# Sums moved to TensorE, projections and sorting moved into other stages, in a four-layer graph kernel

## The chip, the cores and the metric

The kernel runs on one core of a Trainium2 chip. The metric is the device time of one execution in microseconds. The kernel before was run three times: median 3336.72 us, from 3329.15 to 3339.13. One further execution was profiled.

Engines are named as the profile names them: PE is TensorE (PEld its weight loads), DVE is VectorE, ACT is ScalarE, POOL is GpSimd, SP is SyncE, which here only issues DMAs.

## What is computed

A graph of N = 2708 nodes with 128 features passes through four layers. Each has the form x = x + layer(relu(layernorm(x)), adj); everything is fp32. The adjacency `adj` is 2708 x 2708 with some five entries in a row.

```python
# layer 0: graph convolution with symmetric scaling
fc = h @ W + b;  d = adj.sum(1)
x += (adj * d**-.5[:, None] * d**-.5[None, :]) @ fc
# layer 1: attention; here d = 128 "heads" of width h = 8
q = (h @ Wq.T).reshape(d, n, 8)          # k and v alike
a = einsum('dnh,dmh->dnm', q, k) * d**-.5 + adj + adj
x += einsum('dnm,dmh->dnh', softmax(a, 2), v).reshape(n, 8 * d) @ Wo.T
# layer 2: mean over in-edges, two linear maps, batch norm, relu
# layer 3: gated sum over neighbours
gi = sigmoid(a[None] + b[:, None] + b1) * adj[:, :, None]
x += einsum('ijf,jg->ig', gi, h) @ weight + bias
```

## The kernel before

**Layer 0** passes twice over the adjacency in tiles of 128 rows (22 tiles, the last of 20 rows). The first pass loads every tile, sums its rows (`deg`), scales `fc` by the inverse root, and already transposes and multiplies the first `STAY = 8` tiles; the second pass loads the other 14 again, transposes them (`turned`, L303) and multiplies (`product`, L469). On DVE, `neighbours` finds the up to 16 entries of each row (value and column), for ten tiles in the first pass and twelve in the second. The layer norm of layer 1 (`normed_rows`) runs behind the second pass and leaves the transposed `hT`.

**Projections and sorting** are a stage of their own. 144 products of 128 x 512 (L641) make q, k and v; ACT (L648) and DVE (L650) evict them in turn into two tiles, and six DMAs store them to `qkv_c` in DRAM. Beside it `in_order` computes each row's place when rows are sorted by their number of neighbours, and 22 indirect DMAs on POOL's queue scatter the records to `list_d` (L612). Rows sorted so need only `ROOM[t]` neighbour slots in tile t, 121 in all.

**The loop over heads** is written out by hand (`manual_schedule`): engines get their instructions in the order of the code. Exp of the small logit is replaced by a polynomial, so a head's attention over all nodes is a matrix of moments: 128 features of k (`fk`) times nine moments by nine values (`y`), summed over nodes (`moments`, L1200), weighted (L1210), and multiplied with the transposed features of q. The transposes (`turn`, L1226) go through the one PSUM bank of `ps_t` and an ACT copy (`fT`, L1228); `evaluate` multiplies (L1238), scales the 81 results per node by the moments of q (L1246, DVE) and sums nine into one (L1252, DVE). A head has six such chunks of up to four row tiles, and features of the next two heads are made beside it by `keys` (mostly POOL), `with_values` (`y`) and `queries` (DVE). After every fourth head `sums` adds the sum of all v (from `prepare`, L806 to L817) on POOL (L824) and stores the group.

In the same loop a generator `first` takes 1.5 steps per chunk. It relays q, k, v by node (`by_node`), loads the sorted records (`sorted_rows`), and then handles the 121 neighbour slots (`from_neighbours`), each in six steps: an indirect load of k and v, the product k times q (`logits`, POOL L930), its sum over the eight components (`summed`, DVE L936), Exp and weight (`weigh`, ACT), weight times v (`values`, DVE L954), and a sum into PSUM by products with the identity (`added`, PE L971):

```python
nc.tensor.matmul(accs[t][:sz, j], ident[:sz, :sz], z[:sz, j].rearrange("p c k -> p (c k)"), ...)
```

When `first` is exhausted, `normalise` (add the neighbours' part, divide) and `project_out` (PE L676, with `woT` from `load_wo`) take its place. **Layers 2 and 3** follow and are not touched.

Of the kernel before, what the change touches and what calls it, by code (L numbers as in the profile page):

```python
# [28 lines left out]
STAY = 8  # L29
# [16 lines left out]
def gnn4_kernel(  # L46
# [82 lines left out]
    def neighbours(t, sz, a, pool, seg0, at48):  # L129
# [41 lines left out]
        )  # L171
        yield
        col = pool.tile([P, KS], FP, name="n_col")
        nc.vector.reduce_sum(col[:sz], hot[:sz], axis=AX.X)
# [80 lines left out]
    pre = ExitStack()  # L255
    bp = pre.enter_context(tc.tile_pool(name="l01", bufs=1))
    hT = bp.tile([C, N], FP, name="hT")
    with ExitStack() as ph:
        lp = ph.enter_context(tc.tile_pool(name="l0", bufs=1))
        hp = ph.enter_context(tc.tile_pool(name="l0_h", bufs=3))  # L260
        np_ = ph.enter_context(tc.tile_pool(name="l0_n", bufs=2))
# [4 lines left out]
        pa = ph.enter_context(tc.tile_pool(name="l0_pa", bufs=1, space=PSUM))  # L266

        def by_head(src, name):

            nat = ap.tile([P, KC, C], FP, name=f"{name}_nat", tag="a_nat")  # L270
            nc.sync.dma_start(nat, src.rearrange("(t p) c -> p t c", p=P))
            dst = bp.tile([P, HEAD, C], FP, name=name)
            for i0, iw in _cuts(KC, 4):
                pt = ps.tile([P, BK], FP, name="w_ps", tag="tr")
                for i in range(iw):
                    nc.tensor.transpose(pt[:, i * P : (i + 1) * P], nat[:, i0 + i], ident)
                c0, cw = i0 * P // HEAD, iw * P // HEAD
                nc.vector.tensor_copy(
                    dst[:, :, c0 : c0 + cw],
                    pt[:, : iw * P].rearrange("p (c h) -> p h c", h=HEAD),  # L280
                )
            return dst
# [5 lines left out]
        def rows_of_adj(t):  # L288
            r0, sz = rows[t]
            a = ap.tile([P, N], FP, name="a_nat", tag="a_nat")  # L290
            nc.sync.dma_start(a[:sz], adj[r0 : r0 + sz])
            return a

        def turned(t, a, both):

            sz = rows[t][1]
            at = tp.tile([P, NT, P], FP, name="a_tr")
# [16 lines left out]
        fc = lp.tile([P, NT, C], FP, name="fc")  # L314
        junk = lp.tile([P, N], BF, name="junk")
        mv = lp.tile([P, NT, 2], FP, name="mv_0")
        nc.gpsimd.memset(mv, 1.0)
        with tc.manual_schedule():
            stay, gone = list(range(STAY)), list(range(STAY, NT))
            order = [t for two in zip(stay, gone) for t in two] + gone[STAY:]  # L320
            early = stay + gone[:2]
            wT = [by_head(w, f"wT{i}") for i, w in enumerate((wq, wk, wv))]
            nat = [rows_of_adj(t) for t in order[:3]]
            for t, (_, sz) in enumerate(rows):
                st = hp.tile([P, nc.vector.BN_STATS_DIM], FP, name="ln_st")
                nc.vector.bn_stats(st[:sz], x_sb[:sz, t])
                nc.vector.bn_aggr(mv[:sz, t], st[:sz])
            rstd = lp.tile([P, NT], FP, name="rstd_0")
            nc.scalar.activation(rstd, mv[:, :, 1], AF.Sqrt, bias=eps)
            nc.vector.reciprocal(rstd, rstd)  # L330
            for t0, tw in _cuts(NT, 4):
# [3 lines left out]
                for t in range(t0, t0 + tw):  # L335
                    sz = rows[t][1]
                    h = hp.tile([P, C], FP, name="h_0", bufs=4)
                    nc.vector.tensor_scalar(
                        h[:sz], x_sb[:sz, t], mv[:sz, t, 0:1], rstd[:sz, t : t + 1],
                        ALU.subtract, ALU.mult,  # L340
                    )
                    nc.scalar.activation(h[:sz], h[:sz], AF.Relu)
                    o = (t - t0) * P
                    nc.tensor.transpose(pt[:, o : o + sz], h[:sz], ident[:sz, :sz])
                nc.scalar.copy(hT[:, s0 : s0 + w], pt[:, :w])
            for t, (r0, sz) in enumerate(rows):
                pf = pm.tile([P, C], FP, name="fc_ps", tag="mm")
                nc.tensor.matmul(pf[:sz], hT[:, r0 : r0 + sz], w0_sb, start=True, stop=False)
                nc.tensor.matmul(pf[:sz], ones[0:1, :sz], b0_sb, start=False, stop=True)
                nc.scalar.copy(fc[:sz, t], pf[:sz])  # L350

            sums0 = [pa.tile([P, 4, C], FP, name=f"l0_s{g}") for g in range(-(-STAY // 4))]
# [18 lines left out]
            seg_i = lp.tile([P, SEG, 8], I32, name="seg_i")  # L371
            nc.gpsimd.iota(seg_i, pattern=[[seg_w, SEG], [0, 8]], base=0, channel_multiplier=0)
            seg0 = lp.tile([P, CAND], FP, name="seg0")
            nc.gpsimd.tensor_copy(seg0, seg_i.rearrange("p s e -> p (s e)"))
            at_i = lp.tile([P, CAND], I32, name="at_i")
            nc.gpsimd.iota(at_i, pattern=[[1, CAND]], base=0, channel_multiplier=0)
            at48 = lp.tile([P, CAND], FP, name="at48")
            nc.gpsimd.tensor_copy(at48, at_i)
            found = []

            def look(n):
                for _ in range(n):
                    while found and next(found[0], "done") == "done":
                        found.pop(0)

            seen = []
            for i, t in enumerate(order):
                r0, sz = rows[t]
                if i + 3 < NT:
                    nat.append(rows_of_adj(order[i + 3]))  # L390
                a = nat[i]
                look(3)
                nc.scalar.activation(
                    junk[:sz], a[:sz], AF.Copy, accum_out=deg[:sz, t : t + 1]
                )
                d = dinv[:sz, t : t + 1]
                nc.scalar.activation(d, deg[:sz, t : t + 1], AF.Sqrt)
                nc.vector.tensor_scalar_add(d, d, 1e-8)
                nc.vector.reciprocal(d, d)
                nc.vector.tensor_scalar_mul(fc[:sz, t], fc[:sz, t], d)  # L400
# [5 lines left out]
                products(8 if t in stay else 14)  # L406
                seen.append(t)
                ready += [(j, t) for j in sorted(there)]
                ready += [(t, m) for m in seen[:-1] if t in stay]
            look(6)  # L410
            nat = [rows_of_adj(t) for t in gone[:3]]
            products(len(ready))
# [6 lines left out]
            rs1 = lp.tile([P, NT], FP, name="rs1")  # L419
            normed = []  # L420

            def normed_rows(t0, tw):

                hg = hp.tile([P, 4, C], FP, name="h_1", bufs=2)
                for t in range(t0, t0 + tw):
                    sz = rows[t][1]
                    st = hp.tile([P, nc.vector.BN_STATS_DIM], FP, name="ln_st")
                    nc.vector.bn_stats(st[:sz], x_sb[:sz, t])
                    nc.vector.bn_aggr(mv[:sz, t], st[:sz])
                yield  # L430
                r = rs1[:, t0 : t0 + tw]
                nc.scalar.activation(r, mv[:, t0 : t0 + tw, 1], AF.Sqrt, bias=eps)
                yield
                nc.vector.reciprocal(r, r)
                for t in range(t0, t0 + tw):
                    sz = rows[t][1]
                    nc.vector.tensor_scalar(
                        hg[:sz, t - t0], x_sb[:sz, t], mv[:sz, t, 0:1], rs1[:sz, t : t + 1],
                        ALU.subtract, ALU.mult,
                    )  # L440
                for t in range(t0, t0 + tw):
                    sz = rows[t][1]
                    nc.scalar.activation(hg[:sz, t - t0], hg[:sz, t - t0], AF.Relu)
                yield
                pt = ps.tile([P, BK], FP, name="ln_ps", tag="tr")
                s0 = rows[t0][0]
                w = rows[t0 + tw - 1][0] + rows[t0 + tw - 1][1] - s0
                for t in range(t0, t0 + tw):
                    sz = rows[t][1]
                    o = (t - t0) * P  # L450
                    nc.tensor.transpose(pt[:, o : o + sz], hg[:sz, t - t0], ident[:sz, :sz])
                nc.scalar.copy(hT[:, s0 : s0 + w], pt[:, :w])
                yield

            def norm(n):
                for _ in range(n):
                    while normed and next(normed[0], "done") == "done":
                        normed.pop(0)

            groups = _cuts(NT, 4)  # L460
            while groups and sum(groups[0]) <= STAY:
                normed.append(normed_rows(*groups.pop(0)))
# [11 lines left out]
            def added(t, po):  # L474
# [5 lines left out]
                if groups and sum(groups[0]) == t + 1:  # L480
                    normed.append(normed_rows(*groups.pop(0)))
# [13 lines left out]
            for t in range(STAY, NT):  # L495
                if t + 3 < NT:
                    nat.append(rows_of_adj(t + 3))
                a = nat[t - STAY]
                sz = rows[t][1]
                if t not in early:  # L500
                    found.append(neighbours(t, sz, a, np_, seg0, at48))
                    look(2)
                there[t] = turned(t, a, False)
                if t - STAY + 1 < STAY:
# [4 lines left out]
                )  # L509
                if t > STAY:  # L510
                    pos[t - 1] = product(t - 1)
                if t - 2 in pos:
                    added(t - 2, pos.pop(t - 2))
                look(3)
                norm(2)
# [5 lines left out]
            while normed:  # L521
                norm(1)

    VW = HEAD + 1
    QKV = 3 * HEAD + 1
# [1244 lines left out]
```

## Time and profile before

| what | value |
|---|---|
| median of three runs | 3336.72 us |
| profiled execution | 3354.19 us |
| its span, first to last instruction | 3352.4 us |
| mean granted clock of PE | 0.89 |
| busy: PE, PEld, DVE, ACT, POOL | 80, 68, 66, 39, 60% |
| first head's weighting (L1210) starts | 562.6 us |
| the 25th, the 105th and the last | 970.4, 2353.4, 2814.4 us |

The profiled execution is 17.5 us slower than the median; its stages are used for working, and its own time is what they add up to. Busy PE in the profile is modelled: a matmul's record reaches to the end of its pipeline, so distances between starts say more than durations. In a row of costly groups stand the line, engine and operation, output and inputs with their shapes, the count, then busy time in us and mean duration in ns, and last the idle time of that engine just before, with what ended it. In a table by stage, each engine has its busy time and, in brackets, its instructions.

### The profile page before, as it was taken

To read this page: it belongs to the slowest core of one execution; us is meant where nothing else is said; L and a number is where in the kernel's file an instruction comes from. 1 tells how busy PE (TensorE), PEld (TensorE's weight loads), DVE (VectorE), ACT (ScalarE), POOL (GpSimd) and SP (SyncE) were. 2 spreads that over 40 slices of the span, in tenths; PEclk is the share of its full clock that TensorE was granted. 3 is DMA by queue.
4 is the path that set the end of the run, shared out by engine and by line. 5 is a ranking of instruction groups with operands and counts; after the bars stand their busy time and mean duration, and the time that the engine had idled before them with its cause. 6 is when DMAs were issued, how large, how long until landed. Compare 5 with 4: busy or idle time off the path is not lost. (4 is left out here: it accounts for less than half of the span.)

```text
span 3352.4 us, 50866 instructions
## 1 busy us (share of the span) xinstructions
PE 2691.7 (80%) x17781; PEld 2273.0 (68%) x17781; DVE 2202.7 (66%) x5135; ACT 1314.8 (39%) x3127; POOL 2009.3 (60%) x2263
## 2 busy tenths in 40 slices
PE   6477884888789999999999999999888897796044
PEld 4476543777788887888888788877777886443033
DVE  3868753666678888888888788887666675213222
ACT  3485462555544444444444444444322232102010
POOL 0111115555588888888988888889656663000775
PEclk6688896999999999999999999999888999895565
DMA  3452274777743333333334333343465712541322
GB/s 113 175 227 93 76 326 128 208 214 206 211 131 114 125 125 127 128 132 128 119 138 139 126 141 125 137 143 121 94 148 143 166 48 64 193 176 56 106 83 61
DMA packets 312741, 462.08 MB, mean 138 GB/s; under 512 B 159650, under 2 KB 234404, under 8 KB 289330
## 3 DMA queue, kind: packets, MB, share of 16 engines
q1 hardware_dynamic: 280870, 289.79, 28.3%
q0 software_dynamic: 31600, 168.86, 14.7%
q8 instruction: 148, 2.42, 0.3%
q14 instruction: 123, 1.01, 0.1%
HBM read 344.89 MB, written 113.67 MB: 137 GB/s over the span
## 5 line engine op out<-in xcount | busy, mean ns | idle before, releaser
L1238 PE MATMUL g_ps<-mw,fT 128*128 128x128 f32 x5632 | 817.5, 287 | 155.2 <-ACT fT L1228 115.1
L1238 PEld LDWEIGHTS g_ps<-mw,fT 128*128 128x128 f32 x5632 | 715.4, 196 | 290.6 <-ACT fT L1228 178.4
L1228 ACT COPY fT<-f_ps 128x512 f32<-128x512 f32 (+1 forms) x768 | 420.6, 548 | 1216.7 <-PE f_ps L1226 1216.6
L1200 PE MATMUL m_ps<-y,fk 128*128 128x128 f32 (+1 forms) x5632 | 768.2, 280 | 0.0
L1200 PEld LDWEIGHTS m_ps<-y,fk 128*128 128x128 f32 (+1 forms) x5632 | 699.9, 194 | 15.4
L1150 POOL TENSOR_TENSOR y<-bk,raw 128x792 f32<-128x792 f32 x256 | 415.8, 1624 | 432.1 <-ACT y L1181 420.3
L1246 DVE TENSOR_TENSOR z<-g_ps,bq 128x324 f32<-128x324 f32 (+1 forms) x768 | 355.6, 463 | 435.0 <-PE g_ps L1238 433.6
L1226 PE MATMUL f_ps<-ident,fq 128*128 128x128 f32 x2816 | 441.6, 276 | 14.4 <-DVE v_sum L817 9.3
L1252 DVE TENSOR_REDUCE o_raw<-z 128x36 f32<-128x324 f32 (+1 forms) x768 | 355.8, 463 | 26.4
L1150 POOL TENSOR_TENSOR fk<-bk,raw 128x352 f32<-128x352 f32 (+1 forms) x384 | 357.7, 955 | 0.1
L1226 PEld LDWEIGHTS f_ps<-ident,fq 128*128 128x128 f32 x2816 | 340.2, 144 | 16.2 <-DVE v_sum L817 10.6
L1150 POOL TENSOR_TENSOR fk<-raw,bk 128x352 f32<-128x352 f32 (+1 forms) x512 | 312.6, 640 | 3.1 <-ACT bk L719 2.3
L1147 DVE TENSOR_TENSOR fq<-bq,kq_ps 128x528 f32<-128x528 f32 (+1 forms) x512 | 288.2, 605 | 0.0
L930 POOL TENSOR_TENSOR c_z<-c_kv,c_q 128x1024 f32<-128x1024 f32 (+1 forms) x121 | 284.2, 2349 | 2.2 <-DMA c_kv<-kv_n,srt 1.4
L971 PE MATMUL v_ps<-c_v,ident 128*128 128x512 f32 (+1 forms) x484 | 233.3, 605 | 15.3 <-ACT c_acc L986 15.3
L1591 POOL DMA_INDIRECT g<-gate_d,srt x121 | 120.4, 995 | 110.2 <-issue 109.0
L1147 DVE TENSOR_TENSOR fq<-kq_ps,bq 128x352 f32<-128x352 f32 (+1 forms) x512 | 171.9, 378 | 0.0
L155 POOL CAST n_fl<-n_ci 128x40 f32<-128x40 int32 (+1 forms) x22 | 4.8, 218 | 251.9 <-DVE n_ci L138 251.9
L936 DVE TENSOR_REDUCE c_c<-c_z 128x128 f32<-128x1024 f32 (+1 forms) x121 | 147.5, 1219 | 3.4 <-POOL c_z L930 3.2
L954 DVE TENSOR_TENSOR c_v<-c_kv,c_c 128x1024 f32<-128x1024 f32 (+1 forms) x121 | 146.7, 1212 | 0.0
L971 PEld LDWEIGHTS v_ps<-c_v,ident 128*128 128x128 f32 (+1 forms) x484 | 82.0, 189 | 79.1 <-issue 58.8
L915 POOL DMA_INDIRECT c_kv<-kv_n,srt x121 | 117.8, 974 | 23.1 <-issue 9.6
(290 smaller groups left out, 3714.1 us busy)
## 6 DMA issues: line engine op xcount, KB each, us to landing
a_nat<-in_adj_dram SPq DMA_DIRECT2D x34, 1354.0 KB
qkv_c<-qkv SPq DMA_DIRECT2D x5, 6400.0 KB
a<-in_adj_dram SPq DMA_DIRECT2D x21, 1354.0 KB
kv_n<-n_kv SPq DMA_DIRECT2D x16, 1344.0 KB
o_g<-o_raw SPq DMA_DIRECT2D x32, 396.0 KB
q_n<-n_q SPq DMA_DIRECT2D x16, 672.0 KB
o_cr<-o_c SPq DMA_DIRECT2D x21, 512.0 KB
r_raw<-o_g SPq DMA_DIRECT2D x22, 396.0 KB
```

Source lines behind the costliest of these rows:

```text
L930: nc.gpsimd.tensor_tensor(zs[b][:sz], kvs[b][:sz, 0, :, 0], qs[t][:sz], ALU.mult)
L936: nc.vector.reduce_sum(cs[b][:sz], zs.pop(b)[:sz], axis=AX.X)
L954: nc.vector.tensor_tensor(z[:sz], kv[:sz, 0, :, 1].rearrange("p (j c) k -> p j c k", j=2), c.rearrange("p (j c) -> p j c", j=2)[:, :, :, None]
L971: nc.tensor.matmul(accs[t][:sz, j], ident[:sz, :sz], z[:sz, j].rearrange("p c k -> p (c k)"), start=s0 == 0, stop=s0 == ROOM[t] - 1,)
L1147: nc.vector.tensor_tensor(o, x, y, ALU.mult)
L1150: nc.gpsimd.tensor_tensor(o, x, y, ALU.mult)
L1200: nc.tensor.matmul(pms[d][:, :P], fks[d][:sz, t], ys[d, h][:sz, m * VW * B_ALL : m * VW * B_ALL + P], start=t == 0, stop=t == NT - 1,)
L1226: nc.tensor.transpose(pt[:, m], fqs[d][:, t0 + m], ident)
L1228: nc.scalar.copy(fts[d, c][:, :n], pt[:, :n])
L1238: nc.tensor.matmul(pg[:, m], ft[:, m], mws[d], start=True, stop=True,)
L1246: nc.vector.tensor_tensor(z[:, :n], pg[:, :n, : B_ALL * VW].rearrange("p t (k b) -> p t k b", k=VW), bqs[d % 2][:, t0 : t0 + n, None, :B_A ...
L1252: nc.vector.reduce_sum(ros[g][:, t0 : t0 + n, i], z[:, :n], axis=AX.X,)
```

## The change

- `STAY` becomes 6, so the second pass has 16 tiles. Loads of the adjacency run four tiles ahead, and two tiles of the first pass lie between groups of the first layer norm. Norms subtract and scale on POOL, and ACT scales `fc`.
- Projections move into the second pass: when two row tiles of x are complete, `row_group` norms and transposes them, and `projected` makes q, k and v of one row tile with 24 products of 128 columns, evicts four of them at a time, and stores the tile. The stage of its own goes.
- `in_order` moves into the loop and takes its steps beside those of `by_node`; one scatter each two steps.
- `evaluate` writes the scaled results of half a head into one tile `z`, laid out by the nine moments, and `add_up` sums the nine with products with the identity, once in a head, for the second half of the head before and the first half of this one. Two ACT copies take the sums from PSUM, through the bank of `ps_m`.
- `logits` writes its product by component, and `summed` adds the eight components with products with the identity, through the bank of `ps_t`; Exp reads PSUM.
- The sum of all v is made by products with ones in `all_values` from the relaid tiles, and enters each node's result by a product with a row of ones (`vrow`) that opens the sum over neighbours; the store adds N to the denominator. `sums` goes.
- One more pair of features goes from POOL to DVE, `fT` has two buffers instead of three, `c_z`, `c_v` and `z` get a pool of their own, `load_wo` runs when normalising begins, and in `neighbours` three adds on POOL halve the last sum before DVE reduces it.

```diff
-STAY = 8
+STAY = 6
 def neighbours(t, sz, a, pool, seg0, at48):
...
+        while w % 2 == 0:
+            w //= 2
+            nc.gpsimd.tensor_tensor(
+                hot[:sz, :, :w], hot[:sz, :, :w], hot[:sz, :, w : 2 * w], ALU.add
+            )
...
-        nc.vector.reduce_sum(col[:sz], hot[:sz], axis=AX.X)
+        nc.vector.reduce_sum(col[:sz], hot[:sz, :, :w], axis=AX.X)
...
+            early = stay + gone[STAY + 1 :: 2][:4]
...
+            for n, (t0, tw) in enumerate(_cuts(NT, 4)):
+                turned_rows(t0, tw, scaled(t0, tw))
+                if n in (1, 3):
+                    front(n // 2, None)
...
+            def projected(t):
+                r0, sz = rows[t]
+                ot = ots[t % 2]
+                for i in range(3):
+                    for e0 in range(0, HEAD, 4):
+                        pq = pa.tile([P, 4, P], FP, name="qkv_ps", tag="s")
+                        for e in range(4):
+                            nc.tensor.matmul(
+                                pq[:, e, :sz], wT[i][:, e0 + e], hT[:, r0 : r0 + sz],
+                                start=True, stop=True,
+                            )
+                        yield
+                        scale = (C**-0.5, 1.0, 1.0)[i]
+                        to = ot[:, :sz, i * HEAD + e0 : i * HEAD + e0 + 4]
+                        src = pq[:, :, :sz].rearrange("p e r -> p r e")
+                        turns[0] += 1
+                        if turns[0] % 2:
+                            nc.scalar.mul(to, src, scale)
+                        else:
+                            nc.vector.tensor_scalar_mul(to, src, scale)
+                nc.sync.dma_start(qkv_c[:, r0 : r0 + sz], ot[:, :sz])
+                yield
+            def row_group(t0, tw):
+                stats(t0, tw)
+                yield
+                spread(t0, tw)
+                yield
+                hg = scaled(t0, tw)
+                yield
+                turned_rows(t0, tw, hg)
+                yield
+                for t in range(t0, t0 + tw):
+                    yield from projected(t)
...
             for t in range(STAY, NT):
...
+                go(1)
                 there[t] = turned(t, a, False)
+                go(2)
...
+                go(3)
                 if t > STAY:
                     pos[t - 1] = product(t - 1)
+                go(2)
...
-                norm(2)
+                go(3)
...
-                        pq = pm.tile([P, BK], FP, name="qkv_ps", tag="mm")
-                        nc.tensor.matmul(
-                            pq[:, :cw], wT[i][:, e], hT[:, c0 : c0 + cw], start=True, stop=True
-                        )
...
-                    m, of = (mul2, kh2) if w == 6 and h else (mul, kh)
+                    m, of = (mul2, kh2) if w == 6 else (mul, kh)
...
-            nc.gpsimd.tensor_tensor(
-                ro, ro, vs[:, None].to_broadcast([P, NT, GRP, VW]), ALU.add
-            )
+        def all_values(kv, j):
+            pt = ps_t.tile([P, BK], FP, name="v_t", tag="tr")
+            w = 2 * GRP * HEAD
+            to = pt[0:1, :w].rearrange("p (j i k) -> p j i k", j=2, k=HEAD)
+            for t, (_, sz) in enumerate(rows):
+                nc.tensor.matmul(
+                    to, ones[:sz, 0:1], kv[:sz, t, :, :, 1], start=t == 0, stop=t == NT - 1
+                )
+            nc.scalar.copy(vrow[:, (j // 2) * w : (j // 2 + 1) * w], pt[0:1, :w])
...
+                yield
+                yield
+        def side_by_side(a, b):
+            for _ in a:
+                next(b, None)
+                yield
+            yield from b
...
             def summed(b):
-                cs[b] = c_two[:, b % 2, 0]
-                nc.vector.reduce_sum(cs[b][:sz], zs.pop(b)[:sz], axis=AX.X)
+                z = zs.pop(b)
+                cs[b] = ps_t.tile([P, BK], FP, name="c_l", tag="tr")[:, :C]
+                for k in range(HEAD):
+                    nc.tensor.matmul(
+                        cs[b][:sz], ident[:sz, :sz], z[:sz, k],
+                        start=k == 0, stop=k == HEAD - 1,
+                    )
...
                 if s0 == 0:
                     accs[t] = ps_v.tile([P, 2, BK], FP, name="v_ps")
+                    for j in range(2):
+                        nc.tensor.matmul(
+                            accs[t][:sz, j],
+                            ones[0:1, :sz],
+                            vrow[:, j * BK : (j + 1) * BK],
+                            start=True,
+                            stop=False,
+                        )
...
-        first = chain(by_node(), sorted_rows(), from_neighbours())
+        first = chain(side_by_side(by_node(), in_order()), sorted_rows(), from_neighbours())
...
         def evaluate(d, c):
-            z = tm.tile([P, 4, VW, B_ALL], FP, name="z")
+            if t0 == parts[h][0]:
+                zt[d, h] = tz.tile([P, B_ALL, TM, VW], FP, name="z")
+            m0 = t0 - parts[h][0]
             nc.vector.tensor_tensor(
-                z[:, :n],
+                zt[d, h][:, :, m0 : m0 + n].rearrange("p b t k -> p t k b"),
                 pg[:, :n, : B_ALL * VW].rearrange("p t (k b) -> p t k b", k=VW),
                 bqs[d % 2][:, t0 : t0 + n, None, :B_ALL].to_broadcast([P, n, VW, B_ALL]),
                 ALU.mult,
             )
-            nc.vector.reduce_sum(
-                ros[g][:, t0 : t0 + n, i],
-                z[:, :n],
-                axis=AX.X,
-            )
+        def add_up(which):
+            which = [(d, h) for d, h in which if 0 <= d < D]
+            ps = ps_m.tile([P, BK], FP, name="o_ps", tag="m_ps")
+            at = 0
+            for d, h in which:
+                T = parts[h][1] - parts[h][0]
+                z = zt.pop((d, h))
+                for b in range(B_ALL):
+                    nc.tensor.matmul(
+                        ps[:, at : at + T * VW],
+                        ident,
+                        z[:, b, :T],
+                        start=b == 0,
+                        stop=b == B_ALL - 1,
+                    )
+                at += T * VW
...
+                nc.scalar.copy(
+                    ros[g][:, t0:t1, i],
+                    ps[:, at : at + T * VW].rearrange("p (t k) -> p t k", k=VW),
+                )
...
+                    if c == NCH - 1:
+                        add_up([(d - 1, 1), (d, 0)])
```

## The prediction

> **What bounds the kernel now.** I read the stages first, cut at the starts of the work that names them: both passes over the adjacency, projections and sorting (to 563), 24 heads beside the relayout (to 970), 80 heads beside the neighbours (to 2353), 24 heads beside normalising (to 2829), layers 2 and 3. "Head" below means one pass of the loop over the 128 heads; its start is L1210, which runs once per head.
>
> ```profile
> core 0: us, PE busy (x) PEld busy (x) DVE busy (x) ACT busy (x) POOL busy (x), PEclk, DMA share, GB/s
> 0.00:211.00 211.00, 124.99 (x658) 107.35 (x659) 123.58 (x400) 99.93 (x178) 28.51 (x90) 0.68 0.49 180
> 211.00:380.00 169.00, 127.47 (x954) 116.88 (x953) 132.78 (x406) 103.84 (x188) 29.51 (x62) 0.87 0.24 85
> 380.00:563.00 183.00, 125.77 (x354) 63.95 (x352) 91.03 (x144) 79.40 (x92) 43.89 (x57) 0.82 0.57 225
> 563.00:970.00 407.00, 338.48 (x2664) 318.09 (x2664) 263.82 (x636) 221.05 (x497) 238.99 (x321) 0.94 0.70 192
> 970.00:2353.00 1383.00, 1295.39 (x9348) 1117.01 (x9349) 1143.84 (x2459) 600.35 (x1619) 1209.61 (x1261) 0.99 0.37 129
> 2353.00:2829.00 476.00, 402.78 (x2919) 378.79 (x2918) 312.86 (x700) 149.68 (x385) 283.66 (x303) 0.94 0.46 110
> ```
>
> The long stage has PE at 94%, POOL at 87, DVE at 83. Busy PE is modelled, so I ask next what rate PE keeps where nothing holds it: weight loads of one head in the timeline.
>
> ```profile
> 1505.77 0.97 PEld L1238 LDWEIGHTS g_ps<-mw,fT 128*128 128x128 f32 x8 [0.91 <-ACT fT L1228]
> 1506.65 0.47 PEld L1226 LDWEIGHTS f_ps<-ident,fq 128*128 128x128 f32 x4
> 1507.09 0.97 PEld L1200 LDWEIGHTS m_ps<-y,fk 128*128 128x128 f32 x8
> ...
> 1511.28 0.19 PEld L971 LDWEIGHTS v_ps<-c_v,ident 128*128 128x128 f32 x1 [0.24 <-issue]
> 1511.71 0.19 PEld L971 LDWEIGHTS v_ps<-c_v,ident 128*128 128x128 f32 x1 [0.24 <-issue]
> ```
>
> Eight loads take 0.88 us and four take 0.44: 0.11 us per instruction of 128 columns. One of 512 columns takes 0.43. L1238 has 5632 instructions for 2816 products, so an fp32 product is two; a transpose (L1226, 2816) is one. A head is then 44 + 44 + 22 = 110 instructions, 12.2 us. A neighbour (L971, four wide ones) is 1.72 us; 121 neighbours over 80 heads are 1.5 a head, 2.6 us. PE has to work 14.8 us of the 1383/80 = 17.3 us that a head takes: **86% dense**, and 2.5 us a head are all that better order could win.
>
> The operations that the change replaces are these:
>
> ```profile
> L1252 DVE TENSOR_REDUCE o_raw<-z 128x36 f32<-128x324 f32 (+1 forms) x768 | 355.8, 463 | 26.4
> L936 DVE TENSOR_REDUCE c_c<-c_z 128x128 f32<-128x1024 f32 (+1 forms) x121 | 147.5, 1219 | 3.4 <-POOL c_z L930 3.2
> L612 POOL DMA_INDIRECT list_d<-rec,s_at x22 | 21.3, 966 | 133.5 <-DMA list_d<-rec,s_at 99.3 <-DVE s_at L609 29.2 <-DMA n_raw<-qkv_c 5.0
> ```
>
> The first two run on DVE, which itself idles 435 us before L1246 for PE (433.6 in the list of waits). DVE follows PE, not the reverse.
>
> **What the Trainium skill says.** Perfetto Trace Analysis, Identifying the Most-Contended Engine: matmul busy time judges TensorE badly, busy weight loads better. It agrees: 81% of loads against 94% of matmuls in the long stage, my count lies between. TensorE: Matmul & The Clock Gate, LDWEIGHTS: a load takes its columns divided by 1.2 in ns, 107 for 128; the trace has 110. FP8 and Floating Point Precision, TensorE Precision Notes: true fp32 is four passes; the trace shows two records per product, each 0.84 ns a column, so twice the price of the single record that a transpose leaves. VectorE: DVE Perf Modes, the mode table: the 1x mode takes any stride; no run here shows it for a strided fp32 write.
>
> **The change, part by part.**
>
> *Heads' sums.* Goes: L1252, 356 us of DVE. Comes: 18 products per head of 99 columns with the identity as weights, 128 x 18 x 2 = 4608 instructions. By columns alone each is 99 x 0.87 = 0.086 us; by its weight load up to 0.11. I take 0.107: 3.85 us a head, 493 in all (396 to 507). Two ACT copies a head like L1181 (0.37 us) cost nothing: ACT is at 43%. The result tile shares `ps_m`'s one bank with the moments, so the next head's first moments wait for those copies; 8 + 4 PE instructions (1.3 us) lie between. The products stand in the one chunk without moments, where PE now waits for `fT`, so they fill some 0.7 us.
>
> *Neighbours' sums.* Goes: L936, 148 us of DVE. Comes: 8 products of 128 columns, 16 x 0.11 = 1.78 us per neighbour, 215 us, 2.7 a head. They need `ps_t`'s one bank between two transposes: each waits for the last `fT` copy (0.55) and the next transposes for the Exp (0.3). `c_z` and `z` are written with strides; between no change and double on POOL (2.35 us each) and DVE (0.46). I take none, since freed time covers the double: POOL would come to some 17 us and DVE to 13 in a head of 23.
>
> *Sum of v.* Goes: L806 (52 us DVE), L824 (60 POOL), 128 small instructions. Comes: 704 instructions of 64 columns in the relayout stage, 704 x 0.056 = 39 us (78 if a load of 0.11 counts), and 88 wide ones, 88 x 0.43 = 38 us, with the neighbours: 0.5 a head. The pair moved from POOL to DVE (0.7 us a head) hides behind PE.
>
> *Sorting beside the relayout.* The 22 scatters at L612 go from 410.9 to 535.5, 5.7 us apart, each waiting on POOL for the one before. They keep that wait, now with `keys`, `y` and scatter queued behind it. The loop hands one out each 2 steps, 1.33 chunks, 4.3 us; 22 x 1.4 = 30 us too slow, of which POOL's lead hides some: 20.
>
> *Layer 0.* Projections go from 288 wide instructions (112.7 us) to 1056 of 128 columns (117 us) inside the second pass. That pass has 16 tiles instead of 14: 16 x 66 x 0.11 = 116, together 233 us of PE. DVE and ACT add 66 evictions each of 1.0 us (L648, L650). SP's loads of adjacency stand behind 22 stores of q, k, v, four tiles ahead of use, so I count no wait. Three engines near 200 us in one order: at the long stage's density 233/0.87 = 268. The first pass ends 13 sooner, two tiles lying beside the norm; then 18 us from the last row to its projection, and 40 to the first head (now 68 from L641's end, of which sorting 28). 198 + 268 + 18 + 40 = 524 instead of 563: **-38** (-110 if pass two stays near 200; +20). The tournament of adds in `neighbours` (some 1.4 us on POOL, 22 times) lies on an engine 17% busy there.
>
> *Sum.* 80 heads: 14.8 + 3.85 + 2.7 + 0.5 = 21.8 us of PE, with 1.6 us of waits (0.8 to 2.5) 23.4, against 17.3: **+489**. Relayout: 24 x (12.2 + 3.85 + 1.6) = 424, plus 1.6 a head is 462, plus 20 for scatters and 20 for loads of `raw` that still come late, against 407: **+95**. Last 24 heads: 293 of PE now plus L676's 352 x 0.235 = 83 make 376 of 476; plus 92 is 468, and at 88% 531: **+55**. The last sum after the loop: +5. `woT` is now loaded when normalising begins; its transposes stand in PE's queue behind a load that took 3.6 us (510.75 to 514.36 in the timeline): +4. With layer 0, **+610**. Layers 2 and 3 stay. The profiled execution's own time, 3354.2 (2 outside its span), becomes 3964; it lies 17.5 above the median of the runs, so I say **3947**.
>
> **Rivals.** *PE takes the work into its holes.* The loop from 563 to 2829 has 1562 + 208 + 83 + 14 = 1867 us of PE work in 2266. With 493 + 215 + 38 + 39 - 14 = 771 more it is 2638 if wholly dense, +372, and layer 0 gives its 110: 3600; at 97% dense 3680. For it: the new products lie where PE waits. Against: beside the neighbours PE already had their wide products to fill holes with, and 14% stayed.
>
> *New waits take over.* If the single banks of `ps_t` and `ps_m` cost a copy (0.8 us) at each of 1.5 neighbours and at each sum, a head grows 2 us: +210 on 104 heads, 4150.
>
> *It gets faster.* The mechanism would be that an identity product costs one instruction, as a transpose does. Then 4608 + 1936 halve to 350 us, the 399 us of holes hold them, and only layer 0 counts: 3337 - 38 to - 110, about 3260. It decides below some 0.06 us per instruction. L971 speaks against it: an identity product too, and 484 instructions for 242.
>
> That the sums aren't on PE at all is excluded by the order of instructions: 18 products `o_ps` per head and 8 `c_l` per neighbour stand there.
>
> **The numbers.** Likeliest case 0.75 with 3740 to 4100; PE filled to the brim 0.12, below 3740; new waits 0.10, above 4100; faster 0.02; no change 0.01. Range 3740 to 4110. A measurement of this kernel can tell about 0.3%.
>
> **What would show it.** Right: the heads beside the neighbours take some 23 us between starts of the weighting, loads of the `o_ps` products are 0.10 to 0.11 us apart, PE's busy share rises above 96% there, DVE's falls to about 45%, the first head starts near 525. Wrong: `o_ps` at 0.06 or less, a head under 20 us, or DVE or POOL still near 85%.

## The result, and the profile after

The changed kernel takes 4039.5 us against 3335.0 us, median against median of four runs each: a ratio of **1.212** (95% interval 1.2095 to 1.2137), 704.5 us slower. The forecast was 3947.

The stages of the changed kernel, cut at the same marks as before: first pass over the adjacency (to 196), second pass with norm and projections inside (to the first head at 581), 24 heads beside the relayout, 80 beside the neighbours, 24 beside normalising, layers 2 and 3.

```profile
core 0: us, PE busy (x) PEld busy (x) DVE busy (x) ACT busy (x) POOL busy (x), PEclk, DMA share, GB/s
0.00:196.00 196.00, 102.34 (x497) 86.78 (x498) 104.72 (x353) 91.42 (x148) 63.03 (x145) 0.77 0.51 187
196.00:480.00 284.00, 220.04 (x1713) 208.23 (x1712) 136.46 (x382) 133.87 (x232) 54.82 (x98) 0.87 0.41 153
480.00:581.00 101.00, 67.63 (x509) 63.77 (x507) 37.21 (x115) 27.67 (x63) 29.71 (x49) 0.80 0.43 146
581.00:1084.00 503.00, 455.21 (x4146) 433.98 (x4146) 246.56 (x535) 233.18 (x554) 223.23 (x314) 0.99 0.57 155
1084.00:3003.00 1919.00, 1849.77 (x14162) 1655.41 (x14161) 913.68 (x1898) 642.58 (x1782) 1090.29 (x1163) 0.99 0.28 94
3003.00:3514.00 511.00, 478.18 (x3682) 458.37 (x3682) 272.24 (x560) 155.18 (x425) 245.69 (x275) 0.98 0.44 104
...
```

In the long stage PE rose from 94% to 96 (1850 of 1919), while DVE fell from 83% to 48 and POOL from 87 to 57. The two engines that were relieved wait. PE had 9348 matmul instructions in this stage before and has 14162 now. The groups that answer to those replaced (line, engine, operation, count, then busy us and mean ns, then idle time just before, with what ended it):

```profile
L1314 DVE TENSOR_TENSOR z<-g_ps,bq 128x324 f32<-128x324 f32 (+1 forms) x768 | 538.3, 701 | 1293.7 <-PE g_ps L1304 1291.7
L1332 PE MATMUL o_ps<-z,ident 128*128 128x99 f32 x4608 | 533.7, 275 | 1.0 <-DVE mw L1279 0.5 <-ACT o_raw L1347 0.5
L991 PE MATMUL c_l<-c_z,ident 128*128 128x128 f32 (+1 forms) x1936 | 245.7, 280 | 55.8 <-POOL bk L1219 47.1 <-ACT fT L1297 6.1 <-POOL c_z L978 2.6
```

DVE's idle time for PE before its multiplication grew from 434 us to 1292. The mean of 275 ns of a product reaches to the end of its pipeline; what PE is held for is the distance between starts, in the timeline:

```profile
1999.50 2.02 PE L991 MATMUL c_l<-c_z,ident 128*128 128x128 f32 x16 [0.15 <-ACT fT L1297]
2001.36 1.06 PE L1304 MATMUL g_ps<-mw,fT 128*128 128x128 f32 x8
...
2009.58 4.16 PE L1332 MATMUL o_ps<-z,ident 128*128 128x99 f32 x36
2013.57 0.63 PE L1304 MATMUL g_ps<-mw,fT 128*128 128x128 f32 x4
```

From the start of the sums to the start of the next group: 36 instructions in 3.99 us, 0.111 each; 16 in 1.86 us, 0.116 each.

### The profile page after: what moved, and what is told of

The parts are those of the page before. It is cut to its first block, busy times and chain, and to the rows that moved or that the text cites. A ratio compares the mean times of both kernels' runs of the same rounds, so it can differ in the third digit from the quotient of the medians.

```text
span 4036.3 us, 66287 instructions
## 1 busy us (share of the span) xinstructions
PE 3475.6 (86%) x25757; PEld 3099.6 (77%) x25757; DVE 1850.1 (46%) x4243; ACT 1348.0 (33%) x3381; POOL 1879.4 (47%) x2213
## 5 line engine op out<-in xcount | busy, mean ns | idle before, releaser
L1314 DVE TENSOR_TENSOR z<-g_ps,bq 128x324 f32<-128x324 f32 (+1 forms) x768 | 538.3, 701 | 1293.7 <-PE g_ps L1304 1291.7
L1304 PE MATMUL g_ps<-mw,fT 128*128 128x128 f32 x5632 | 792.8, 283 | 73.1 <-ACT fT L1297 55.6
L1332 PE MATMUL o_ps<-z,ident 128*128 128x99 f32 x4608 | 533.7, 275 | 1.0 <-DVE mw L1279 0.5
L1332 PEld LDWEIGHTS o_ps<-z,ident 128*128 128x128 f32 x4608 | 525.6, 192 | 1.7 <-DVE mw L1279 1.0
L1295 PEld LDWEIGHTS f_ps<-ident,fq 128*128 128x128 f32 x2816 | 337.5, 143 | 22.4 <-issue 22.1
L991 PE MATMUL c_l<-c_z,ident 128*128 128x128 f32 (+1 forms) x1936 | 245.7, 280 | 55.8 <-POOL bk L1219 47.1
L978 POOL TENSOR_TENSOR c_z<-c_kv,c_q 128x1024 f32<-128x1024 f32 (+1 forms) x121 | 285.4, 2359 | 3.7 <-DMA c_kv<-kv_n,srt 2.9
L991 PEld LDWEIGHTS c_l<-c_z,ident 128*128 128x128 f32 (+1 forms) x1936 | 224.4, 190 | 74.1 <-POOL bk L1219 53.5
L1038 PE MATMUL v_ps<-c_v,ident 128*128 128x512 f32 (+1 forms) x484 | 245.0, 631 | 0.0
L1216 DVE TENSOR_TENSOR fk<-bk,kq_ps 128x528 f32<-128x528 f32 x256 | 168.6, 700 | 108.7 <-POOL bk L1219 103.9
L1219 POOL TENSOR_TENSOR fk<-bk,raw 128x352 f32<-128x352 f32 x256 | 214.8, 852 | 0.3
L1347 ACT COPY o_raw<-o_ps 128x99 f32<-128x99 f32 x256 | 50.3, 251 | 435.5 <-PE o_ps L1332 435.5
```

The source lines that it names most:

```text
L978: nc.gpsimd.tensor_tensor(zs[b][:sz].rearrange("p k c -> p c k"), kvs[b][:sz, 0, :, 0], qs[t][:sz], ALU.mult,)
L991: nc.tensor.matmul(cs[b][:sz], ident[:sz, :sz], z[:sz, k], start=k == 0, stop=k == HEAD - 1,)
L1216: nc.vector.tensor_tensor(o, x, y, ALU.mult)
L1219: nc.gpsimd.tensor_tensor(o, x, y, ALU.mult)
L1295: nc.tensor.transpose(pt[:, m], fqs[d][:, t0 + m], ident)
L1304: nc.tensor.matmul(pg[:, m], ft[:, m], mws[d], start=True, stop=True,)
```

## The experiments

Each kernel was timed in turn with the kernel before, whose medians then lay between 3331.0 and 3335.5 us. The table has, in us of each kernel's profiled execution, the start of the first head (its weighting), the next 24 heads, one head of the 80 beside the neighbours, the 23 starts that follow, and what remains; last the median. L0 is layer 0.

| kernel | first head | 24 heads | one of 80 | last 23 | rest | median |
|---|---|---|---|---|---|---|
| before | 562.6 | 407.7 | 17.29 | 461.0 | 538.0 | 3335.0 |
| after | 580.7 | 503.8 | 23.99 | 511.2 | 521.7 | 4039.5 |
| 1 L0 and projections as before | 562.1 | 503.9 | 23.98 | 513.8 | 523.3 | 4020.2 |
| 2 heads' sums on DVE | 582.6 | 437.7 | 20.11 | 466.8 | 510.5 | 3608.8 |
| 3 neighbours' sums on DVE | 582.0 | 505.6 | 21.39 | 508.9 | 521.2 | 3837.0 |
| 4 both on DVE | 581.7 | 445.1 | 17.63 | 463.7 | 512.7 | 3415.6 |
| 5 no halving adds | 561.5 | 501.6 | 23.97 | 513.7 | 520.1 | 4016.6 |
| 6 before + new L0 and sort | 564.9 | 441.9 | 17.29 | 466.2 | 515.6 | 3370.5 |
| 7 before + moved sort | 536.8 | 444.1 | 17.29 | 463.2 | 516.6 | 3348.0 |
| 8 half the columns in sums | 580.6 | 501.2 | 24.46 | 518.8 | 523.8 | 4081.5 |
| 9 as 7, sort thinly spread | 537.4 | 412.5 | 17.30 | 462.8 | 517.1 | 3311.0 |
| 10 as 6, later transposes | 558.3 | 440.3 | 17.27 | 463.9 | 512.7 | 3361.0 |
| 11 as 9, transposes ahead | 538.7 | 404.8 | 18.85 | 450.0 | 509.3 | 3418.0 |

Layers 2 and 3 take 509 to 524 us everywhere except in the one profiled execution of before (538), though they are the same code. That excess is about what this execution lies above its median (17.5), so the differences of the table are read against the median without the last column.

**1. Only the loop's part of the change.** Layer 0 and the stage of projections are put back; sorting stays in the loop, and so do the halving adds in `neighbours`.

```diff
-STAY = 6
+STAY = 8
...
-            def projected(t):
...
+            for c, (c0, cw) in enumerate(cols):
```

> The changed kernel with layer 0 and the projections of the kernel before (eight tiles kept, projections in a stage of their own), sorting still beside the relayout. Theory: the fused layer 0 brings the first head at 581 us instead of 563, and it would be about 535 without the sorting's tail, so this kernel is some 46 us faster than the changed one: 3993 us, with the loop over heads unchanged (24.0 us a head beside the neighbours). Rival: fusing saves time as I predicted (38 us) and the late first head comes from the new loop's own start: then 4039 us or more.

Measured 4020.2, between the theory and its rival: putting layer 0 back is worth 19 us, all in the first head's start (580.7 to 562.1). The new layer 0 is a loss, not the gain of 38 that I had forecast, and 97% of the 704 us lies elsewhere. The stage of projections lost its sorting here and still did not end sooner than before. The halving adds explain it: kernel 7 below has the same layer 0 without them and starts its first head at 536.8, 25 us sooner. Experiment 5 takes them alone.

**2 to 4. The sums go back to DVE**, the heads' (2), the neighbours' (3), both (4); everything else as changed. The first part of the excerpt stands in 2 and 4, the second in 3 and 4.

```diff
-                    if c == NCH - 1:
-                        add_up([(d - 1, 1), (d, 0)])
+            nc.vector.reduce_sum(ros[g][:, t0 : t0 + n, i], z[:, :n], axis=AX.X)
...
-                cs[b] = ps_t.tile([P, BK], FP, name="c_l", tag="tr")[:, :C]
-                for k in range(HEAD):
...
+                cs[b] = c_two[:, b % 2, 0]
+                nc.vector.reduce_sum(cs[b][:sz], zs.pop(b)[:sz], axis=AX.X)
```

> The changed kernel with the heads' sums back on DVE (multiply and reduce per chunk), all else as changed. Theory (PE is full, so each instruction added to it is paid): 4608 instructions of 0.111 us go, 512 us, of which some 40 come back as waits for fT: 3560 us, range 3520 to 3600; a head beside the neighbours falls from 24.0 to about 20.2 us. Rival (the new waits on single PSUM banks cost, not the instructions): the sums' own products are cheap and the time falls by less than 350 us: above 3690.

> The changed kernel with the neighbours' sums back on DVE, all else as changed. Theory: 1936 instructions of 0.111 us go, 215 us, and with them the wait of these products for POOL (47 us in the list of waits): 3800 us, range 3770 to 3840. Rival (the bank that the sums share with the transposes makes PE wait beyond its work): the time falls by over 300 us, below 3740.

> The changed kernel with both sums back on DVE; the fused layer 0, sorting beside the relayout, and the sum of v by products with ones stay. Theory: the two savings add up, since both are PE work on a full PE: 4039 - 480 - 240 = 3320 us, range 3290 to 3380, about the kernel before. Rival (they share one cause, a wait, that the removal of either one takes away): the sum falls short, and this kernel is above 3420.

Without the heads' sums 3608.8: **431 us** gone, just short of the range, though a head fell to 20.11 as expected. Without the neighbours' 3837.0: **202 us**, within the range. Without both 3415.6: 624, within 10 us of the two added up. So the costs add, as work on one full engine does, and the rival of a shared wait falls. By place, against after: the heads' sums cost 23.99 - 20.11 = 3.88 us in each of the 80 heads, where their 36 instructions by 0.111 are 4.0. Beside the relayout they cost (503.8 - 437.7)/24 = 2.75, and in the last heads 44.4/23 = 1.9. The neighbours' cost 23.99 - 21.39 = 2.60 a head, where 121/80 of them by 16 instructions of 0.111 are 2.69. So in the long stage, where PE is busy 96% of the time in kernels 2 and 3, 97% of either sum's work shows as time. In the other two stages PE is busy 85 and 86% in kernel 2, and 69 and 48% of the heads' work shows.

The fourth kernel stayed 80 us slower than before, above its range, which ends at 3380: other parts of the change lose too. They come next.

**5. The halving adds alone.** DVE reduces all of `hot` again.

```diff
-        while w % 2 == 0:
-            w //= 2
-            nc.gpsimd.tensor_tensor(
-                hot[:sz, :, :w], hot[:sz, :, :w], hot[:sz, :, w : 2 * w], ALU.add
-            )
...
-        nc.vector.reduce_sum(col[:sz], hot[:sz, :, :w], axis=AX.X)
+        nc.vector.reduce_sum(col[:sz], hot[:sz], axis=AX.X)
```

> The changed kernel without the three halving adds on POOL in the neighbour search: DVE reduces 640 to 16 as before. Theory: DVE waits in its own order for those adds (80 us before n_col in the list of waits, 38 in the kernel before), so they lengthen layer 0 by up to 43 us, and part of it is on the path because DVE's queue also holds the norm and the evictions: 4015 us, range 4000 to 4028, with the first head near 557. Rival (the second pass is full of PE work and DVE's wait is hidden, as I predicted): 4039 us within 8.

Measured 4016.6, as expected: the adds cost 22.9 us, 19.2 of them ahead of the first head. This is the idle time of DVE before the reduction, in the lists of waits (waiting, releaser, total us, times, the longest) of before

```profile
DVE n_col L174 <- POOL n_hot L166: 37.8, 22, 1.7
```

and of after:

```profile
DVE n_col L180 <- POOL n_hot L175: 80.4, 22, 3.7
```

Over 22 tiles the reduction itself fell from 18.0 us to 5.2, and DVE's wait for POOL rose by 42.6. POOL has time to spare, but the three adds stand one after another between two instructions of DVE, and what the program puts behind the reduction on DVE comes later too.

**6 and 7. What was moved, on the loop of before.** 7 takes the sorting out of the stage of projections and lets it run beside `by_node`, at the change's pace. 6 has this and the new layer 0 with its fused projections, without the adds.

```diff
-            sort = in_order(so, ps)
...
-                            next(sort, None)
...
-        first = chain(by_node(), sorted_rows(), from_neighbours())
+        first = chain(side_by_side(by_node(), in_order()), sorted_rows(), from_neighbours())
```

> The kernel before with the fused layer 0 (projections inside the second pass, six tiles kept) and the sorting beside the relayout, but with the old neighbour search, the old sums on DVE and the old sum of v. Theory (fusing buys little, because the second pass waits for the chain from a row's product to its norm to its projections): first head near 557, scatters cost the relayout some 10 us: 3340 us, range 3320 to 3355. Rival (the fused layer 0 is worth the predicted 38 us and only the adds hid it): below 3315.

> The kernel before with only the sorting moved beside the relayout. Theory: the first head comes some 16 us sooner (the store of the last projections ends at 511, the scatters at 536), and the scatters' waits on POOL give about 10 of it back in the relayout: 3327 us, range 3318 to 3337. Rival (POOL's queue is what the relayout waits for: 22 scatters of 5.7 us): the relayout loses 20 us or more and the kernel is not faster: 3337 or more.

Neither won. Kernel 6 took 3370.5, above its range and far from its rival; kernel 7 took 3348.0, and both signs of its rival came. Before had 3335.5 beside them. In 7 the first head starts 25.8 us sooner, and the relayout takes 36.4 longer. The first eight heads show where (us between starts of the weighting, worked out of the trace):

```
before  12.7  15.2  19.7  15.2  15.2  21.1  15.2  15.2
7       22.1  21.0  19.8  16.9  25.4  31.0  15.4  20.5
9       15.1  17.0  18.9  15.1  17.5  18.4  15.2  15.2
```

The scatters of kernel 7, seen by their tile (count, shortest, median and longest ns, first and last start; waits in us and times):

```profile
L859 POOL DMA_INDIRECT list_d<-rec,s_at x22: 915/1006/1184, 579.4 to 693.4; - x22
...
  DMA list_d<-rec,s_at: 38.8, 14
...
DMA to landing us min/median/max: 2.2/5.3/7.1
```

They follow one another every 5.4 us (114 over 21). Fourteen of them wait on POOL until the one before has landed, 38.8 us in all, and a head's `y` and features stand behind them in POOL's queue.

The new layer 0 itself costs a further 28.1 us to the first head (564.9 against 536.8), and 22.4 in the medians.

**8. What is a product with the identity paid for?** Nothing but the number of columns is changed: eight of a head's nine terms enter with half their row tiles, so the other half of the rows lacks these terms.

```diff
                 for b in range(B_ALL):
+                    n = T if b == 0 else T // 2
...
-                        ps[:, at : at + T * VW],
+                        ps[:, at : at + n * VW],
                         ident,
-                        z[:, b, :T],
+                        z[:, b, :n],
```

> The changed kernel, in which eight of nine products of each half head move only five row tiles (45 columns instead of 99); the terms of the other row tiles are left out of the sum. Theory (each instruction costs its weight load, 0.11 us): 4039 us within 15. Rival (each costs its columns and a fixed part, 99 x 0.87 + 25 ns = 0.111 too): 4096 instructions fall to 0.064 us, 190 us less: 3850.

Columns are not the price: products of 45 columns start 0.111 us apart on average, as those of 99 do, and the time did not fall. Nor is it a fixed price of any product. In the changed kernel the sum of v multiplies 64 columns, but loads a single column of weights, the ones:

```profile
615.54 2.70 PE L802 MATMUL v_t<-n_kv,ones 128*1 128x64 f32 x44
```

These 704 instructions start 0.056 us apart (median). So what an identity product pays for is the load of its 128 weight columns. This agrees with the Trainium skill (TensorE: Matmul & The Clock Gate, LDWEIGHTS), where a load takes its columns divided by 1.2 in ns, which is 107 for 128.

The measured time fits neither the theory nor the rival: the kernel got 42 us slower. The long stage has a lower granted clock, 0.96 against 0.99:

```profile
1084.00:3003.00 1919.00, 1868.77 (x13912) 1659.97 (x13913) 894.36 (x1861) 631.52 (x1753) 1068.09 (x1142) 0.96 0.28 92
```

It shows where columns are the price: from start to start, the products of 512 columns that sum the neighbours (L1038 in both) take 0.527 us on average where they took 0.462, with medians alike (0.430 and 0.429), so some of them meet a slow clock. 480 of them by 0.065 are 31 of the 42 us; the rest was not followed up. Why the clock falls with emptier products was not tried.

**9. The sort, spread.** As 7, but `in_order` gets a step on every third turn only, so the scatters have landed when the next is due.

```diff
-        first = chain(side_by_side(by_node(), in_order()), sorted_rows(), from_neighbours())
+        first = chain(side_by_side(by_node(), slowly(in_order())), sorted_rows(), from_neighbours())
```

> The kernel before with the sorting beside the relayout, each of its steps three times as far apart (a scatter every six steps, about 10 us, instead of every two). Theory: scatters cost the relayout only where they come faster than the 5.3 us that one takes to land, so POOL no longer waits, the 26 us of the earlier first head stay, and the 22 us of issues on POOL are mostly hidden: 3315 us, range 3305 to 3326. Rival (it is the bank, DVE and POOL work of the sorting itself that the heads pay, not the scatters' pace): the relayout stays 30 us or more longer and the kernel is at 3340 or more.

Measured **3311.0** against 3331.0 of before beside it, as expected; the ratio is 0.994 (0.9922 to 0.9954). It is faster than both kernels, if by little. The same view as for 7:

```profile
L859 POOL DMA_INDIRECT list_d<-rec,s_at x22: 918/1008/1188, 617.6 to 858.3; - x22
...
  DMA list_d<-rec,s_at: 2.0, 4
...
DMA to landing us min/median/max: 4.3/5.6/6.8
```

A scatter lands as late as before, but they start 11.5 us apart. The wait falls from 38.8 us to 2.0, the relayout from 444.1 to 412.5, and the 25 us of the earlier first head stay. Moving the sort was sound; its pace was not.

**10. The fused layer 0, with a gap.** As 6, but three more turns of other work between a group's norm and its transposes.

```diff
                 hg = scaled(t0, tw)
-                yield
+                for _ in range(4):
+                    yield
                 turned_rows(t0, tw, hg)
```

> The kernel before with the fused layer 0 and the sorting beside the relayout (the run of the moves alone), with three more empty steps between a row group's scaling and its transposes, so that other products stand in PE's queue between them. Theory (the fused pass is late because PE reaches the transposes before the chain over DVE, ACT, POOL and ACT has made the normed rows: 41 us of waits): some 20 of it goes, the first head comes near 545 instead of 565: 3350 us, range 3340 to 3362. Rival (PE's work and the tail of projections after the last product set the end; filling a wait only moves it): 3370 within 8, or more.

Measured 3361.0, at the end of its range: 9.4 less than 6 and still 0.9% above before. The first head came to 558, not to 545. PE's waits in the second pass of 6:

```profile
PE ln_ps L394 <- ACT h_g L381: 40.6, 8, 8.7
PE a_ps L305 <- ACT a_tr L310: 8.5, 2, 5.0
PE qkv_ps L505 <- ACT hT L395: 8.2, 8, 5.0
```

And with the gap:

```profile
PE ln_ps L394 <- ACT h_g L381: 23.8, 5, 8.7
PE a_ps L305 <- ACT a_tr L310: 16.8, 3, 8.6
PE qkv_ps L505 <- ACT hT L395: 16.4, 9, 5.7
```

`ln_ps` fell by 16.8 us, the two others rose by 16.5 together. The wait that I took away came back in the list behind other instructions on PE, and the first head starts only 6.6 us sooner. A row's way from product to norm to transpose to projection crosses PE, DVE, POOL and ACT, and each stands in its own order; one gap did not loosen it.

**11. Transposes two chunks ahead.** As 9, and with `ps_t` of two banks, its second taken from `c_c`, which moves to SBUF; features of q asked for earlier. It was to win the waits for `fT` beside the neighbours.

```diff
-                    if c + 1 < NCH:
-                        turn(d, c + 1)
+                    if c + 2 < NCH:
+                        turn(d, c + 2)
...
-                    for _ in range(3 if c < 4 else NCH * 3):
+                    for _ in range(4 if c < 3 else NCH * 3):
...
-            c_two = ps_c.tile([P, 2, S, C], FP, name="c_c")
+            c_two = lp.tile([P, 2, S, C], FP, name="c_c")
```

> As the run with the spread sorting, and the transposes of a head's features issued two chunks ahead of their use instead of one, with two PSUM banks for them (the neighbours' weights go to SBUF to free one). Theory (PE sets the loop, and 115 us of its waits before g_ps are for the fT copy): most of these go, 0.6 to 0.9 us a head, 90 us: 3230 us, range 3200 to 3270, a head beside the neighbours at 16.5 us. Rival (waits only move: PE then waits for z, y or fk instead): less than 30 us below the run with the spread sorting.

Measured 3418.0: 107 us slower than 9. PE's waits before the products with q's features, from 1000 to 2300, in 9

```profile
PE g_ps L1247 <- ACT fT L1237: 33.2, 80, 0.7
PE g_ps L1247 <- DVE mw L1219: 21.5, 17, 1.6
```

and in 11:

```profile
PE g_ps L1246 <- DVE mw L1218: 83.9, 24, 5.5
PE g_ps L1246 <- DVE z L1254: 37.7, 21, 3.9
```

The wait for `fT` is gone, and 122 us of waits for DVE stand where 21 did. DVE has as many instructions in the 80 heads as in 9, but is busy 194 us longer. Nearly all of it lies in the products that read `c_c`, the tile that was moved, first in 9 and then in 11:

```profile
L963 DVE TENSOR_TENSOR c_v<-c_kv,c_c 128x1024 f32<-128x1024 f32 (+1 forms) x121 | 146.5, 1211 | 0.0
L962 DVE TENSOR_TENSOR c_v<-c_kv,c_c 128x1024 f32<-128x1024 f32 (+1 forms) x121 | 302.5, 2500 | 0.0
```

With their weights in SBUF instead of PSUM they take twice as long, 156 us more, and the sum of the weights (`c_den`) 44 more. No other group of DVE changed by over 2 us. So the trace lays the loss to the moved tile; no run has the earlier transposes without it, and whether they would win anything stays open.

**The account.** Heads' sums 431, neighbours' 193 (what 4 adds to 2), halving adds 23, fused layer 0 22 (6 against 7), the sort at its pace 13 (7 against before): 682 of 704.5. The rest, 22, is what 4 has over 6 (45) less the adds: the sum of v, the moved pair of features and the smaller edits to the loop, which no kernel takes alone. By place those 45 are 17 ahead of the first head, where the adds are, 27 in the 80 heads, where the 88 wide products of the sum of v stand, and 3 beside the relayout. None of the parts that were tried alone gained at the change's own settings.

## Why the prediction was right, point by point

The direction and the mechanism held: PE was the bound, the sums are work on PE, and work taken from DVE and POOL bought nothing. The size came out 92 us short: 56 of it in layer 0 and 47 in the 80 heads, less some 13 in the other terms.

- **What bounds it: right.** DVE was relieved of 503 us (L1252 and L936) and POOL of L824, and what they gained in the long stage is idle time: DVE went from 83% busy to 48 while a head grew from 17.3 us to 24.0.
- **Price of an identity product: right.** I took 0.107 for the heads' and 0.11 for the neighbours'; measured 0.111 and 0.116. The rival of one instruction each fell: 4608 and 1936 stand in the trace.
- **80 heads: +536 where I had +489.** PE's work by the measured rates is 12.2 + 4.0 + 2.7 + 2.6 + 0.5 = 22.0 us. The term that was mis-sized is "with 1.6 us of waits": they are 24.0 - 22.0 = 2.0 (before 2.5), and so make up 0.4 of the 0.6 us by which a head came out longer; the rest is the price of the products. I believed that the heads' products would "fill some 0.7 us" of PE's wait for `fT`. In this stage that wait was 35.8 us before, 0.45 a head. In kernel 2, without the heads' products, the list of waits has

```profile
PE g_ps L1304 <- ACT fT L1297: 30.3, 42, 0.7
PE c_l L991 <- POOL bk L1219: 18.8, 40, 0.5
```

and in the changed kernel 1.1 and 47.1. So the wait for `fT` was filled, and the neighbours' sums then waited 28 us longer for POOL. PE's idle time in the stage is 71 us in kernel 2 and 69 after: the wait moved, and nothing was won.
- **24 heads beside the relayout: +96 where I had +95.** Right in the sum by luck, not in its terms: the heads' products cost 66, not 92; the sum of v some 3 (4 against 6), not 39, though its products start 0.056 us apart as I had said; the scatters 36 (in 7), not 20. I had 30 us for these and let POOL's lead hide a third; nothing was hidden.
- **Last heads: +50 where I had +55.** Right, with half of the products absorbed.
- **Layer 0: wrong in sign.** I had -38; the first head starts 18 later. Three terms, by the experiments: the sort's removal -26, near the 28 I had; the halving adds +19, which I put at nothing since they lie "on an engine 17% busy there"; the fused passes +28 where I had -10. I had the last row 268 us after the second pass begins, at the long stage's density. From 201 to the end of the last product at 515 it is 314; from 196 to 480 PE is busy 77% of the time, not 87. The last projection then ends at 551, 36 us after the last product instead of 18. PE stands open for the norms:

```profile
517.61 0.44 PE L400 MATMUL ln_ps<-ident,h_g 128*128 128x128 f32 x2 [2.87 <-ACT h_g L387]
...
534.52 0.33 PE L400 MATMUL ln_ps<-ident,h_g 128*128 128x128 f32 x1 [3.40 <-ACT h_g L387]
...
535.89 8.95 PE L511 MATMUL qkv_ps<-hT,wT 128*128 128x128 f32 x64 [0.37 <-ACT hT L401]
```

Two groups of rows come after the last product, not one. The density of one stage was carried to another whose chain crosses four engines.
- **Last sum and `woT`, +9: not seen.** The rest is 522 us, within the 509 to 524 of all kernels.
- **From profiled to median: right.** The 17.5 us lay in layers 2 and 3 of that one execution.
- **The rivals.** PE filling its holes (3600 to 3680) failed on the long stage, where PE's idle time went only from 87 us to 69. Single banks: PE's idle time ahead of L1332 is 1.0 us in all and ahead of L991 55.8, not 210.

Of the signs that I named, four came: heads of 24.0 us, sums 0.111 apart, PE at 96.4%, DVE at 48. The first head near 525 did not.

## What to carry to other kernels

Before a reduction moves to TensorE, count its instructions by their weight loads: an fp32 product with the identity costs two loads of 128 columns (0.111 us each here, with 45 columns to multiply as with 99), and on an engine 94% full nearly all of it was time. Stages with holes took a part for nothing, so the worth of an edit is measured stage by stage. A small step placed on an idle engine still costs if a busy engine's next instruction waits for it, and a serial chain of DMAs hides only if its pace leaves each the time to land: at 5.4 us apart these cost 36 us, at 11.5 apart 5.

## What the hardware showed unexpectedly

- Products of 45 columns in place of 99 cost PE the same 0.111 us, and the granted clock of the long stage fell from 0.99 to 0.96. The sums' own products did not slow down with it; those of 512 columns did, from 0.462 us to 0.527 on average.
- DVE's multiplication of the same shapes took 701 ns in place of 463 when its fp32 results lie 396 bytes apart (L1314 after, L1246 before). The Trainium skill (VectorE: DVE Perf Modes, the mode table) has the 1x mode, one element a cycle, work for everything; it did work here, but took 1.5 times as long. Kernel 2, which writes the results in a row again, is back at 463. POOL's strided write did not change (2359 ns against 2349).
- Evictions of 512 elements from PSUM took 669 ns on ACT and 688 on DVE when written in runs of four (L521, L523), where those before, written one by one, took 1124 and 1107 (L648, L650). The order of reading changed with it, so the runs of four are not shown to be the cause. I had put either at 1.0 us.
- A DVE product of 1024 columns took 2500 ns on average, from 1214 up to 6639, when its second factor was moved from PSUM to SBUF, and 1211 before (experiment 11). What it meets there was not tried.
